# Stage borders of an eight-block network: tile pools placed by lifetime at two ends of SBUF and PSUM, and DRAM sums zeroed in a later stage

## The chip, the cores and the metric

The kernel runs on one core of one Trainium2 chip. The metric is the device time of one execution in microseconds (us). Before the change three executions took 4508.14, 4526.53 and 4512.35 us; the median is 4512.35. One further execution was profiled and took 4548.0 us; all rows of the profile are from that one. TensorE is called PE, VectorE DVE, ScalarE ACT, GpSimd POOL and SyncE SP.

## The reference, cut to what matters

The input is x, 8 sequences of 512 tokens with 128 features, float32. Four layers follow, each an attention block and a feed-forward block, with a norm ahead of each block and its result added to x:

```python
x = x + L0_attn(norm(x))   # delta rule with short convolutions, two FIR filters, a fusing gate
x = x + L0_ffn(norm(x))    # one of 8 experts for each token, weighted by its probability
x = x + L1_attn(norm(x))   # 4 layers: 4 local heads, 4 linear heads, and an MLP each
x = x + L1_ffn(norm(x))    # 8 experts choose their tokens; LayerNorm, MLP, scatter-add
x = x + L2_attn(norm(x))   # gated delta rule, gate, output projection, GELU
x = x + L2_ffn(norm(x))    # 2 layers of windowed attention with rotary positions, and a GLU
x = x + L3_attn(norm(x))   # chunked memory with decay
x = x + L3_ffn(norm(x))    # two of 8 experts for each token
```

What has to start at zero: the expert blocks L1_ffn and L3_ffn add rows into buffers in DRAM (`acc1` and `acc`, two each), which are then added to x.

## The kernel before

**Layout.** x stays in SBUF as 32 tiles of 128 tokens x 128 features (NT = 32), in eight batches of 512 tokens (NB = 8), one for each sequence. `build` (L2035) loads eight constants, calls `load_x` (L74: eight loads of 256 KB on SP's queue) and `row_buffers` (L79), then runs the eight stages as methods one after the other, and stores x.

**DRAM buffers.** `row_buffers` makes `rows_in` (rows that experts gather), `rows_out`, `acc` and `acc1`. It clears a 128 x 1024 tile z on POOL and writes it with POOL-issued DMAs into the extra rows of `rows_in` and over all four sum buffers: 1 + 18 DMAs, 8.5 MB for the 18.

**Stages and pools.** Each stage opens its tile pools in SBUF and PSUM at its begin and closes them at its end. Pools lie on a stack from the left end. So the first pool of a stage gets the addresses of the first pool of the stage before, and a new tile has to wait until whatever lay at its address is done, on every engine and DMA queue that used it. The stages are emitted in program order, and a scheduler then fixes the order of each engine's own queue. An engine executes its queue strictly in order.

The pools that the change names: `a0`, `a0g` and `a0l` of L0_attn (weights and whole-stage tiles; fuse weights; work tiles), with the PSUM rings psA, psC, psD and psF; `f0`, `f0w` and `f0h` of L0_ffn; `a1`, `a1w` and `a1l` of L1_attn; `f1`, `f1s`, `f1w` and `f1h` of L1_ffn (`f1s` holds the norms ahead of the routing); `a2` and `a2l` of L2_attn; `rt` of `route_in` (L611, norm and routing scores of L0_ffn and L3_ffn); `f3`, `f3w` and `f3h` of L3_ffn.

**The norm.** `norm` (L61 to L72) takes one batch of four tiles: four bn_stats (L65) and four bn_aggr (L67) on DVE, `r = var + eps` (L69) on DVE, `r ** -0.5` (L70) on POOL, and four scalings (L72) on DVE.

**Start, L0_attn (L207).** The q, k, v and o projections, the convolution weights and two masks are loaded into `a0`, the fuse weights into `a0g` with their cleared tiles, and softplus of `logit_temp` (L196 to L198, three ACT steps) is worked out for the gate's `tm`. `L0_values` then does, for each batch: norm (xn), transposes, v projection (L276), a causal convolution of four taps on DVE (L187, L189), silu on ACT (L190), and a FIR filter of five taps on DVE (L282, L284).

**L0_ffn (L640) to L1_attn (L694).** The last step of L0_ffn gathers 32 tiles `yg` by indirect DMAs issued on POOL (L609) and adds each, times its probability, to x on DVE (L692). L1_attn opens with three casts of constants, 18 memsets on POOL (L727 to L729: vl, vg, mt, cn, three sets), a norm of each batch into y, and then runs 32 items (4 layers x 8 sequences). `together` (L1535) interleaves four parts of different items by their due times: projection, maxima, values and MLP. Weights of the next layer are loaded through the SP queue one layer ahead (pool `a1w`, two buffers). `L1_maxima` reduces the scores ps_s in PSUM (L845, L847 on PE) into mt by three DVE reduces for an item (L851, L852, L854). With the last layer's MLP, y is finished (L978) and POOL adds it to x (L982).

**L1_attn to L1_ffn (L983).** For each of the eight batches L1_ffn norms x to xn, transposes it and multiplies by the gate, adds xn to x on POOL (L1016), norms xn to yn, and stores yn to `rows_in` (L1019). The norms' tiles are in `f1s`, two buffers each. Then come the choice of tokens, the experts with their scatter-adds into `acc1`, and `add_sums` (L1163): 16 loads `sum` on SP, added to x alternately by DVE and POOL (L1170).

**L1_ffn to L2_attn (L1320).** L2_attn loads some twenty weights and constants, clears the buffers of its triangular inverse (L204, invH), makes two casts (L1346) and `na` (L1348, with an ACT table), and `L2_proj` does for each batch: norm of x to xi, norm of xi to hn, two row operations (L1369, L1370), an RMS norm, transposes, and four projections with convolutions (L1384).

**L3.** L3_attn runs the eight sequences one after the other; L3_ffn loads Wgate, bgate and b3, routes by `route_in`, runs the experts with scatter-adds into `acc`, and ends with `add_sums`.

Of the kernel before, what the change touches and what calls it, by code (L numbers as in the profile page):

```python
# [9 lines left out]
F32 = mybir.dt.float32  # L10
# [5 lines left out]
P = 128  # L16
D = 128
L = 512
TPB = L // P
# [9 lines left out]
class Net:  # L29
# [49 lines left out]
    def row_buffers(self, ctx):  # L79


        tc, nc = self.tc, self.nc
        NR = self.NT * P
        N = ((NR - 8) // 256 + 8) * 256
        dram = ctx.enter_context(tc.tile_pool(name="dram", bufs=1, space=bass.MemoryType.DRAM))
        self.rows_in = dram.tile([NR + P, D], F32, name="rows_in")
        self.rows_out = dram.tile([N, D], F32, name="rows_out")
        self.acc = [dram.tile([NR + P, D], F32, name=f"acc{i}") for i in range(2)]
        self.acc1 = [dram.tile([NR, D], F32, name=f"acc1{i}") for i in range(2)]
        with tc.tile_pool(name="zero", bufs=1) as zp:  # L90
            z = zp.tile([P, 8, D], F32, name="z")
            nc.gpsimd.memset(z, 0.0)
            nc.gpsimd.dma_start(self.rows_in[NR:, :], z[:, 0, :])
            for a in self.acc1 + self.acc:
                N = a.shape[0]
                for n in range(0, N, 8 * P):
                    m = min(8, (N - n) // P)
                    nc.gpsimd.dma_start(a[n : n + m * P, :].rearrange("(t p) d -> p t d", p=P), z[:, :m, :])

# [106 lines left out]
    def L0_attn(self):  # L206
# [4 lines left out]
        H, E, NL = 4, 32, 2  # L211
        with ExitStack() as es:
            cp = es.enter_context(tc.tile_pool(name="a0", bufs=1))
            w = {k: self.load(cp, f"L0_attn_{k}_proj_w", [D, D]) for k in ("q", "k", "v", "o")}
# [10 lines left out]
            ll = cp.tile([P, NT, D], F32, name="ll")  # L225
            gc = es.enter_context(tc.tile_pool(name="a0g", bufs=1))
            lp = es.enter_context(tc.tile_pool(name="a0l", bufs=1))
# [23 lines left out]
            self.ps = es.enter_context(tc.tile_pool(name="ps", bufs=1, space=bass.MemoryType.PSUM))  # L251
            self.rings = {"psA": 1, "psC": 1, "psD": 2, "psF": 2}
            for b in range(NB):
# [356 lines left out]

    def route_in(self, wg, E):  # L611

        nc, NB = self.nc, self.NB
        ps = self.psum("ps_sp")
        with self.tc.tile_pool(name="rt", bufs=3) as rp:
            for b in range(NB):
                xn = rp.tile([P, TPB, D], F32, name="xn")
                self.norm(rp, xn, self.x[:, b * TPB : (b + 1) * TPB, :])
                nc.sync.dma_start(self.seq_rows(self.rows_in, b), xn)
                hT = rp.tile([D, L], F32, name="hT")  # L620
                self.transpose4(hT, xn)
                for t in range(TPB):
                    n = b * TPB + t
                    nc.tensor.matmul(ps[:, n * E : (n + 1) * E], self.cols(hT, t), wg, start=True, stop=True)
        return ps[:, : self.NT * E].rearrange("p (n e) -> p n e", e=E)
# [13 lines left out]
    def L0_ffn(self):  # L639
# [4 lines left out]
        with ExitStack() as es:  # L644
            cp = es.enter_context(tc.tile_pool(name="f0", bufs=1))
            wp = es.enter_context(tc.tile_pool(name="f0w", bufs=5))
            hp = es.enter_context(tc.tile_pool(name="f0h", bufs=2))
            es.enter_context(self.banks(4))
            wr = self.load(cp, "L0_ffn_Wr", [D, E])
            br = self.load_row(cp, "L0_ffn_br", E)  # L650
            lg = self.route_in(wr, E)
            rt = cp.tile([P, NT, E], F32, name="rt")
            nc.vector.tensor_tensor(rt, lg, bc(br, 1, NT), ALU.add)
            nc.scalar.activation(rt, rt, AF.Sigmoid)
            mx = cp.tile([P, NT], F32, name="mx")
            nc.vector.tensor_reduce(mx, rt, AX.X, ALU.max)
# [3 lines left out]
            TB = BS // P  # L660
            idx = self.token_lists(pos, NBLK * TB, cp)
            places = cp.tile([P, NT], mybir.dt.int32, name="places")
            nc.vector.tensor_copy(places, pos)

            st = [{} for _ in range(NBLK)]
            for i in range(NBLK + 2):
# [11 lines left out]
                if 0 <= i - 2 < NBLK:  # L678
                    j = i - 2
                    w, hid = st[j]["w"], st[j]["hid"]  # L680
                    po = self.psum("po")
                    for t in range(TB):
                        for f in range(FC):
                            nc.tensor.matmul(self.cols(po, t), self.cols(hid[:, f, :], t), self.cols(w, FC + f), start=(f == 0), stop=(f == FC - 1))
                    y = hp.tile([P, TB, D], F32, name="y", bufs=3)
                    nc.vector.tensor_copy(y.rearrange("p t d -> p (t d)"), po[:, :BS])
                    nc.sync.dma_start(self.rows_out[j * BS : (j + 1) * BS, :].rearrange("(t p) d -> p t d", p=P), y)
            for n in range(NT):
                yg = hp.tile([P, D], F32, name="yg", bufs=8)
                self.gather(yg, self.rows_out[:, :], places[:, n : n + 1])  # L690
# [3 lines left out]
    def L1_attn(self):  # L694
# [6 lines left out]
        with ExitStack() as es:  # L701
# [36 lines left out]
            for n in range(-2, N + 1):  # L738
                m = n + 2
                if m < N:  # L740
                    i = order[m][0]
# [22 lines left out]
    def single(self, tag, name):  # L764
        return self.ps.tile([P, 512], F32, tag=tag, name=name, bufs=self.rings.get(tag, 2))

# [217 lines left out]
    def L1_ffn(self):  # L984
# [8 lines left out]
        with ExitStack() as es:  # L993
            cp = es.enter_context(tc.tile_pool(name="f1", bufs=1))
            sp = es.enter_context(tc.tile_pool(name="f1s", bufs=2))
            wp = es.enter_context(tc.tile_pool(name="f1w", bufs=3))
# [323 lines left out]
    def L2_attn(self):  # L1320
# [5 lines left out]
        with ExitStack() as es:  # L1326
            cp = es.enter_context(tc.tile_pool(name="a2", bufs=1))
            lp = es.enter_context(tc.tile_pool(name="a2l", bufs=1))
# [32 lines left out]
    def L2_proj(self, s, w, cw, row, col, c, lp):  # L1361
        nc = self.nc
        H = 4
        xb = self.x[:, s["b"] * TPB : (s["b"] + 1) * TPB, :]
        s["xi"] = xi = lp.tile([P, TPB, D], F32, name="xi", bufs=4)
        self.norm(lp, xi, xb)
        hn = lp.tile([P, TPB, D], F32, name="hn")
        self.norm(lp, hn, xi)
        nc.vector.tensor_tensor(hn, hn, bc(row["ln1_g"], 1, TPB), ALU.mult)  # L1369
# [109 lines left out]
    def L2_out(self, s, w, row, col, c, lp):  # L1479
# [40 lines left out]
        hn = lp.tile([P, TPB, D], F32, name="hm")  # L1520
        self.norm(lp, hn, xi)
        yield
# [331 lines left out]
    def L3_ffn(self):  # L1854
# [5 lines left out]
        with ExitStack() as es:  # L1860
            cp = es.enter_context(tc.tile_pool(name="f3", bufs=1))
            wp = es.enter_context(tc.tile_pool(name="f3w", bufs=5))
            hp = es.enter_context(tc.tile_pool(name="f3h", bufs=2))
            es.enter_context(self.banks(8))
            wg = self.load(cp, "L3_ffn_Wgate", [D, E])
            bg = self.load_row(cp, "L3_ffn_bgate", E)
            b3 = self.load(cp, "L3_ffn_b3", [E, D])
            lg = self.route_in(wg, E)
            g = cp.tile([P, NT, E], F32, name="g")
# [168 lines left out]
def build(nc, T, stages, NB, src, dst):  # L2038
    with tile.TileContext(nc) as tc:
        with ExitStack() as ctx:  # L2040
# [11 lines left out]
            net.load_x(src)  # L2052
            net.row_buffers(ctx)
            for s in stages:
                with ExitStack() as es:
# [22 lines left out]
```

## Time and profile before

| What | Value |
|---|---|
| Executions | 4508.14, 4526.53, 4512.35 us; median 4512.35 |
| Profiled execution | 4548.0 us, of which the span of instructions is 4546.2 |
| Mean granted clock of PE | 0.813 |
| Start: window 10 to 40 us | DMA engines 0.94 to 1.03 busy, PE without work until 49.91 |
| L0_ffn to L1_attn | last gathered add 1039.72, PE's next transposes 1068.38 (idle 72.92) |
| L1_attn, window 1840 to 2050 | PE busy 197.32, DVE 102.19, clock 0.98 |
| L1_attn to L1_ffn | last y 2135.95, last of eight norm chains and its row store about 2191 |
| L1_ffn to L2_attn | first sum load 2419.83, PE's first transposes 2457.77 (idle 18.19) |
| L2_attn to L2_ffn | loads 3158.69 to 3174.9, PE on again at 3177.15 (idle 22.63) |
| End | last sums and stores 4511.44 to 4546 |

How to read it: a timeline row gives start, duration, engine, line, operation, output<-inputs with shapes, and in brackets the idle time of that engine just before and what ended it; several like instructions are drawn into one row with their number behind an x. "PEld" is PE's weight load, "SPq" an issue of a DMA on SP. A window row gives each engine's busy time (with the number of its instructions), then the clock granted to PE, the busy share of the 16 DMA engines and GB/s. Line numbers are those of the kernel before; the changed kernel's are 5 higher from L107 on, 6 to 12 higher further down.

### The profile page before, as it was taken

How to read it: one execution, taken by the hardware profiler on the slowest of the kernel's cores; microseconds unless marked ns; L12 is line 12 of the kernel's file. 1: busy time of each engine (PE TensorE's matmuls, PEld its weight loads, DVE VectorE, ACT ScalarE, POOL GpSimd, SP SyncE). 2: the span in 40 equal slices, each digit the busy share in tenths (PEclk: the TensorE clock that was granted, in tenths of full speed). 3: DMA queues.
4: the chain of work that ended last, by engine and by line, in shares of the span. 5: the costliest groups of instructions: out<-in, count | busy, mean ns of one | idle time of the engine just before them, and what ended most of it. 6: DMA issues, size and time to landing. Idle time of an engine off the chain costs nothing.

```text
span 4546.2 us, 104956 instructions
## 1 busy us (share of the span) xinstructions
PE 3767.2 (83%) x45952; PEld 2718.9 (60%) x45952; DVE 2392.7 (53%) x5895; ACT 1687.4 (37%) x2541; POOL 1589.5 (35%) x1575
## 2 busy tenths in 40 slices
PE   3899998575999999997466899995899899986998
PEld 1687776463656565654343677774466566665665
DVE  5445555416454545443615566643766777655333
ACT  2233443112444444442012444532466555631221
POOL 2122221353121112122255334331554554523774
PEclk7565566587999999996576787865899999997998
DMA  3300000150000000000022000001000000001554
GB/s 108 87 3 3 2 3 2 57 151 11 2 5 6 4 7 1 1 1 22 13 50 59 3 3 2 3 3 40 1 1 1 1 1 1 1 13 60 147 147 122
DMA packets 111227, 130.78 MB, mean 29 GB/s; under 512 B 18352, under 2 KB 90497, under 8 KB 110769
## 3 DMA queue, kind: packets, MB, share of 16 engines
q0 software_dynamic: 33184, 76.14, 6.5%
q1 hardware_dynamic: 77584, 47.93, 3.8%
q8 instruction: 361, 5.91, 0.5%
q14 instruction: 98, 0.80, 0.1%
HBM read 96.83 MB, written 27.20 MB: 27 GB/s over the span
## 4 chain that ended last, share of the span: by engine, by line
PE 59%; DVE 18%; ACT 7%; POOL 6%; issue 5%; DMA 2%; another core or an unknown queue 2%; POOLq 0%; SPq 0%; DVEq 0%; ACTq 0%
PE ps_h L971 3%; PE po L977 3%; PE ps_a L1315 2%; POOL nm_r L70 2%; PE ps_qk L1648 2%; PE pd L1279 2%; PE ps_tr L773 2%; PE px L1203 2%; PE pg L1911 2%; PE pz L1210 2%; DVE nm_st L65 2%; PE ps_s L845 2%; DVE mt L854 2%; PE po L1298 1%
## 5 line engine op out<-in xcount | busy, mean ns | idle before, releaser
L70 POOL TENSOR_TENSOR nm_r<-nm_r,mhalf 128x4 f32<-128x4 f32 x168 | 173.0, 1030 | 403.7 <-DVE nm_r L69 399.6
L1660 POOL TENSOR_TENSOR r<-r,rot 128x512 f32<-128x512 f32 x128 | 162.6, 1271 | 303.8 <-DVE rot L1659 248.1
L978 DVE TENSOR_TENSOR y<-y,po 128x512 f32<-128x512 f32 x32 | 22.0, 687 | 313.1 <-PE po L977 313.1
L876 POOL TENSOR_TENSOR cn<-cx,rc 64x448 f32<-64x448 f32 x32 | 37.6, 1174 | 412.9 <-DVE rc L874 412.9
L971 PE MATMUL ps_h<-hTm,w 128*128 128x512 f32 x256 | 163.5, 724 | 11.4 <-ACT hid L972 4.7
L927 ACT ACTIVATE pT<-ps_s 128x2048 f32<-128x2048 f32 x64 | 106.5, 1664 | 169.9 <-PE ps_s L925 169.9
L1648 PE MATMUL ps_qk<-wqkv,hTq 128*128 128x512 f32 x256 | 147.7, 672 | 18.2 <-DVE hTq L1640 7.7
L1199 POOL TENSOR_TENSOR iM<-iN,c_lvl 128x512 f32<-128x512 f32 x64 | 87.1, 1370 | 198.5 <-PE px L1203 185.8
L923 PE MATMUL ps_s<-qa,kT 32*128 32x256 f32 (+1 forms) x1024 | 149.8, 409 | 0.6 <-DVE mt L854 0.3
L609 POOL DMA_INDIRECT xr<-rows_in,tl_idx x124 | 118.7, 957 | 75.7 <-PE pt L634 20.9
L606 POOL DMA_INDIRECT acc<-y,tl_idx x78 | 124.8, 1601 | 45.1 <-DVE y L1921 21.4
L972 ACT ACTIVATE hid<-ps_h,b 128x512 f32<-128x512 f32 x128 | 88.0, 687 | 129.2 <-PE ps_h L971 128.0
L977 PEld LDWEIGHTS po<-w,hid 128*128 128x128 f32 x1024 | 122.2, 199 | 20.9 <-ACT hid L972 20.9
L977 PE MATMUL po<-w,hid 128*128 128x128 f32 x1024 | 128.3, 286 | 5.8 <-ACT hid L972 1.6
L773 PE MATMUL ps_tr<-ident,xn 128*128 128x128 f32 x160 | 29.8, 315 | 124.5 <-DVE xn L72 124.5
L1678 POOL TENSOR_TENSOR r<-r,rn 128x512 f32<-128x512 f32 x128 | 129.1, 1042 | 1.9
L1210 PE MATMUL pz<-iTT,iX 32*32 32x32 f32 x8192 | 103.8, 209 | 25.8 <-issue 19.3
L1210 PEld LDWEIGHTS pz<-iTT,iX 32*32 32x32 f32 x8192 | 92.6, 121 | 54.0 <-issue 36.7
L1650 ACT ACTIVATE sq<-ps_qk 128x512 f32<-128x512 f32 x128 | 75.8, 592 | 121.2 <-PE ps_qk L1648 121.2
L854 DVE TENSOR_REDUCE mt<-ps_s 128x8 f32<-128x2048 f32 x32 | 73.4, 2293 | 88.4 <-PE ps_s L847 88.4
L1203 PEld LDWEIGHTS px<-iT,iM 32*32 32x32 f32 x8192 | 96.2, 126 | 36.6 <-issue 23.1
L1203 PE MATMUL px<-iT,iM 32*32 32x32 f32 x8192 | 106.2, 214 | 5.6 <-issue 3.4
(672 smaller groups left out, 10765.3 us busy)
## 6 DMA issues: line engine op xcount, KB each, us to landing
acc<-z POOLq DMA_DIRECT2D x16, 512.0 KB
fcur<-in_L_attn_fir_cur SPq DMA_DIRECT2D x32, 256.0 KB
sum<-acc SPq DMA_DIRECT2D x32, 256.0 KB
rows_in<-xn SPq DMA_DIRECT2D x16, 256.0 KB
rows_out<-y SPq DMA_DIRECT2D x23, 128.0 KB
x<-in_L_attn_hidden_states SPq DMA_DIRECT2D x8, 256.0 KB
fprev<-in_L_attn_fir_prev SPq DMA_DIRECT2D x8, 256.0 KB
w<-in_L_attn_W SPq DMA_DIRECT2D x8, 256.0 KB
```

What stands on the lines that cost most here:

```text
L70: nc.gpsimd.tensor_tensor(r, r, self.mhalf[:, :G], ALU.pow)
L606: self.nc.gpsimd.indirect_dma_start(out=dst, out_offset=bass.IndirectOffsetOnAxis(ap=idx, axis=0), in_=src, in_offset=None, compute_op=ALU ...
L773: nc.tensor.transpose(self.cols(ps, g), src[:, g, :], self.ident)
L854: nc.vector.tensor_reduce(m4, s4, AX.X, ALU.max, negate=True)
L923: nc.tensor.matmul(ss[:, h, n * 256 : n * 256 + W], kT[R[h], k * P : (k + 1) * P], qa[R[h], k * P : k * P + W], start=True, stop=False)
L971: nc.tensor.matmul(ps, self.cols(w["w1"], f), hT, start=True, stop=True)
L977: nc.tensor.matmul(self.cols(po, t), self.cols(hid[:, f, :], t), w["w2"][:, f, :], start=(f == 0), stop=(f == FC - 1))
L1203: nc.tensor.matmul(px[p, g * B : (g + 1) * B], nm[p, g, :], Ti[p, g, :], start=True, stop=True)
L1210: nc.tensor.matmul(pz[p, g * B : (g + 1) * B], X[p, g, :], TT[p, g, :], start=True, stop=True)
L1648: nc.tensor.matmul(ps, self.cols(hT, t), w["qkv"][:, j, :], start=True, stop=True)
L1660: nc.gpsimd.tensor_tensor(r3, r3, m, ALU.add)
L1678: nc.gpsimd.tensor_tensor(r3, r3, bc(rn[:, j, t, :], 2, E), ALU.mult)
```

## The change

It edits where pools are opened and which pool a tile comes from, and moves the zeroing of the sums; no arithmetic is changed.

- `row_buffers` clears only a 128 x 128 tile and the extra rows of `rows_in`. The new `zero_sums` clears a 128 x 8 x 128 tile z on POOL and writes it over `acc1` and `acc` by 18 DMAs on SP's queue; L1_attn calls it with its pool `a1` when its loop comes to n = 1.
- These pools open at the right end: `a0`, `a0g`; a PSUM pool "psl" of its own for L0_attn's ring psF; `f0y`, new, for L0_ffn's y, yg, mx and places; `f1s`; `a2` and a new `a2x` with the norms' tiles and xi of L2_attn; `rt` (for L3_ffn), `f3`, `f3w`, `f3h`.
- L0_ffn's Wr and br come from the pool of constants.
- `single` takes a ring given as (buffers, pool).

```diff
         with tc.tile_pool(name="zero", bufs=1) as zp:
-            z = zp.tile([P, 8, D], F32, name="z")
+            z = zp.tile([P, D], F32, name="z")
             nc.gpsimd.memset(z, 0.0)
-            nc.gpsimd.dma_start(self.rows_in[NR:, :], z[:, 0, :])
-            for a in self.acc1 + self.acc:
-                N = a.shape[0]
-                for n in range(0, N, 8 * P):
-                    m = min(8, (N - n) // P)
-                    nc.gpsimd.dma_start(a[n : n + m * P, :].rearrange("(t p) d -> p t d", p=P), z[:, :m, :])
+            nc.gpsimd.dma_start(self.rows_in[NR:, :], z)
+
+    def zero_sums(self, pool):
+        nc = self.nc
+        z = pool.tile([P, 8, D], F32, name="z")
+        nc.gpsimd.memset(z, 0.0)
+        for a in self.acc1 + self.acc:
+            N = a.shape[0]
+            for n in range(0, N, 8 * P):
+                m = min(8, (N - n) // P)
+                nc.sync.dma_start(a[n : n + m * P, :].rearrange("(t p) d -> p t d", p=P), z[:, :m, :])
...
-            cp = es.enter_context(tc.tile_pool(name="a0", bufs=1))
+            cp = es.enter_context(tc.tile_pool(name="a0", side="right", bufs=1))
...
-            gc = es.enter_context(tc.tile_pool(name="a0g", bufs=1))
+            gc = es.enter_context(tc.tile_pool(name="a0g", side="right", bufs=1))
...
-            self.rings = {"psA": 1, "psC": 1, "psD": 2, "psF": 2}
+            last = es.enter_context(tc.tile_pool(name="psl", side="right", bufs=1, space=bass.MemoryType.PSUM))
+            self.rings = {"psA": 1, "psC": 1, "psD": 2, "psF": (2, last)}
...
+            yp = es.enter_context(tc.tile_pool(name="f0y", side="right", bufs=3))
             es.enter_context(self.banks(4))
-            wr = self.load(cp, "L0_ffn_Wr", [D, E])
-            br = self.load_row(cp, "L0_ffn_br", E)
+            wr = self.load(self.const, "L0_ffn_Wr", [D, E])
+            br = self.load_row(self.const, "L0_ffn_br", E)
...
-                yg = hp.tile([P, D], F32, name="yg", bufs=8)
+                yg = yp.tile([P, D], F32, name="yg", bufs=8)
...
             for n in range(-2, N + 1):
                 m = n + 2
+                if n == 1:
+                    self.zero_sums(cp)
...
-            sp = es.enter_context(tc.tile_pool(name="f1s", bufs=2))
+            sp = es.enter_context(tc.tile_pool(name="f1s", side="right", bufs=2))
...
-            cp = es.enter_context(tc.tile_pool(name="a2", bufs=1))
+            cp = es.enter_context(tc.tile_pool(name="a2", side="right", bufs=1))
+            self.late = es.enter_context(tc.tile_pool(name="a2x", side="right", bufs=1))
...
-        s["xi"] = xi = lp.tile([P, TPB, D], F32, name="xi", bufs=4)
-        self.norm(lp, xi, xb)
+        s["xi"] = xi = self.late.tile([P, TPB, D], F32, name="xi", bufs=4)
+        self.norm(self.late, xi, xb)
...
-            cp = es.enter_context(tc.tile_pool(name="f3", bufs=1))
-            wp = es.enter_context(tc.tile_pool(name="f3w", bufs=5))
-            hp = es.enter_context(tc.tile_pool(name="f3h", bufs=2))
+            cp = es.enter_context(tc.tile_pool(name="f3", side="right", bufs=1))
+            wp = es.enter_context(tc.tile_pool(name="f3w", side="right", bufs=5))
+            hp = es.enter_context(tc.tile_pool(name="f3h", side="right", bufs=2))
```

## Prediction, made blind

> **What bounds the kernel now.** I read the page's busy shares and its chain first, then windows over each stage border, then the timelines at those borders, and last how the two programs order each engine's instructions.
>
> ```profile
> span 4546.2 us, 104956 instructions
> PE 3767.2 (83%) x45952; PEld 2718.9 (60%) x45952; DVE 2392.7 (53%) x5895; ACT 1687.4 (37%) x2541; POOL 1589.5 (35%) x1575
> PE 59%; DVE 18%; ACT 7%; POOL 6%; issue 5%; DMA 2%; another core or an unknown queue 2%; POOLq 0%; SPq 0%; DVEq 0%; ACTq 0%
> ```
>
> TensorE carries the chain inside the stages; DVE, ACT and POOL carry most of the rest, and the borders are where TensorE stands. The change adds no arithmetic: TensorE's and DVE's instructions stay the same in number, ACT gets three table loads, SP 18 DMAs that POOL loses. TensorE's order is nearly untouched; the other engines' moves lie almost all at borders, so the working goes border by border. The profiled run took 4548.0 us (span 4546.2), 35.7 above the median 4512.35 of the three runs shown; I sum differences from the profiled execution and take them off that median.
>
> **A. The start.** Windows (busy PE, PEld, DVE, ACT, POOL, then clock, DMA share, GB/s) and timeline rows:
>
> ```profile
> 10.00:20.00 10.00, 0.00 (x0) 0.00 (x0) 1.32 (x9) 0.00 (x0) 5.00 (x7) 1.00 1.03 310
> 20.00:30.00 10.00, 0.00 (x0) 0.00 (x0) 0.87 (x4) 0.00 (x0) 5.40 (x8) 1.00 1.03 301
> 2.91 8.86 POOL L98 DMA_DIRECT2D acc<-z  x10
> 4.51 32.69 SPq L77 DMA_DIRECT2D x<-in_L_attn_hidden_states  x8
> 46.66 0.43 SPq L150 DMA_DIRECT2D L_attn_v_proj_w<-in_L_attn_v_proj_w  x1
> 59.28 0.49 DVE L187 TENSOR_SCALAR cv_acc<-cv_pre,L_attn_v_conv_w 128x512 f32<-128x512 f32 x1
> ```
>
> The DMA engines are full with 8.5 MB of zeros (L98); each of the 8 loads of x takes 4.09 us (32.69 / 8), and all compute engines stand. The weights of L0_attn follow on SP, so the first convolution starts at 59.28; from there DVE is busy for 58.33 of 65 us (60 to 125).
> Afterwards only 64 KB of zeros precede x, and the projection weights come directly after x, ahead of the fuse weights. Alone, loads of x's shape go at 1.07 us each (sum<-acc, 8 in 8.56) to 1.35 (out_x<-x, 5 in 6.74): x is issued by 4.51 + 8.6 to 10.8 = 13.1 to 15.3. v_proj is third after it (0.47 apart), the v conv weights seventh; a small load lands about 2.0 us after its issue, so they are there at 16.4 to 18.6 and 18.4 to 20.5. The first norms need 7.5 (first x) to 14.5 (second xn, at the 3.1 us a batch of 50.66 to 57.05). v_proj, 2.05 with its copy and wait as before, is hidden in that: first convolution at 19.5, a gain of 39.8 (38.7 to 40.8). Against it: DVE has by then done 2 xn, 4 statistics, 4 aggregates and the three tm steps less than before, 2.5 us that now fall into its full stretch. On ACT the logit_temp chain (47.08 to 49.03 before, in the idle start) now stands between the first and second silu, waits for a load issued 23rd after x (lands about 26) and brings 3 table loads of 1.28; ACT was idle 4.0 and 4.7 us around those silus, so I take 1 of the 3.84. Sum **-36**; bounds -28 (slow loads, all table loads and waits paid) and -41.
>
> **B. L0_attn to L0_ffn (820 to 855).** The order doesn't change; Wr is loaded earlier, but was there in time (issued 820.97, used 826.41). 0.
>
> **C. L0_ffn to L1_attn (995 to 1068).** After the last gathered add (1039.72), 18 memsets hold POOL from 1040.26 to 1045.5, and the first norm's power waits for them (1045.51). Ten move ahead of the 32 gathers, into POOL's idle time before 998.5 (the gathers may start 0.6 later); eight short ones stay, 1.9 us, so the power starts at about 1040.1. The statistics of four batches go between adds that the gathers pace at 1.25 us. -5.4 + 0.6 = **-5** (-3 to -6).
> The zeroing comes back here: 18 SP DMAs after the first two layers' weights, 8.5 MB at the start's 300 GB/s = 28 us, about 1045 to 1075. Queued behind them on SP is only the third layer's first load, wanted at 1237 before. No other data moves then; only instruction fetch (queue q8, 5.91 MB in the whole run) shares the engines. No row shows it squeezed: 0 to +5, I take **+1**, since TensorE starts only at 1068.
>
> **D. L1_attn to L1_ffn (1950 to 2190).** The interesting border.
>
> ```profile
> 2135.95 0.69 DVE L978 TENSOR_TENSOR y<-y,po 128x512 f32<-128x512 f32 x1 [19.56 <-PE po L977]
> 2136.55 0.87 DVE L65 BATCH_NORM_STATS2 nm_st<-x 128x6 f32<-128x128 f32 x4
> 2152.81 1.12 DVE L72 TENSOR_SCALAR xn<-x,nm_mv,nm_r 128x128 f32<-128x128 f32 x4 [1.19 <-POOL nm_r L70]
> ```
>
> After the last y, eight batches take 6.67 us each of DVE and POOL norms. With f1s on the far side, both norms of batches 0 and 1 and the statistics of batch 2 move into L1_attn. xn of batch 2 then waits only for the transposes of batch 0 behind the last po, about 2137.3 instead of 2152.81: **-15.5**.
> But they go into DVE's queue just ahead of the maxima mt (L851, L852) of items whose seconds count:
>
> ```profile
> 1957.70 0.68 DVE L851 TENSOR_REDUCE mt<-ps_s 128x4 f32<-128x512 f32 x1
> 1958.30 1.22 DVE L852 TENSOR_REDUCE mt<-ps_s 128x4 f32<-128x1024 f32 x1
> 1960.34 0.71 PE L845 MATMUL ps_s<-kT,qT 32*128 32x256 f32 x8
> 1962.40 2.29 DVE L854 TENSOR_REDUCE mt<-ps_s 128x8 f32<-128x2048 f32 x1 [2.88 <-PE ps_s L847]
> ```
>
> TensorE's third group of scores (1960.34) overwrites the PSUM that the second mt reads, and waits for its end (1959.52): slack 0.8. Inserted ahead: a wait for POOL's x 0.3, statistics 0.95, aggregate and r 0.5, power on POOL 1.2 and 0.6 behind cn, xn 1.05, statistics 0.8, aggregate, r and power 1.75, the first yn 0.25: 7.4. Less 0.8, TensorE stands 6.6 us, at 1960 and again at 1991; the third insertion (statistics only, 1.8) costs 1.0. Everything behind TensorE in this stage waits with it (197.32 of 210 us busy). **+14.2**; at least +4 if the gaps of the rest (6%) take some back, and no less, since DVE cannot pass its own queue.
> Then the clock:
>
> ```profile
> 1084.00:1092.00 8.00, 7.95 (x38) 4.51 (x42) 5.02 (x11) 1.37 (x2) 2.74 (x2) 0.50 0.00 0
> 1100.00:1108.00 8.00, 7.47 (x93) 4.69 (x91) 4.79 (x8) 3.51 (x4) 1.18 (x1) 1.00 0.00 0
> 2060.00:2070.00 10.00, 9.76 (x78) 4.93 (x79) 2.31 (x3) 7.34 (x8) 0.34 (x1) 0.66 0.01 2
> ```
>
> The granted clock stands at 0.50 after idle stretches and takes up to 30 us to come back (1068 to 1100), or dips only briefly (0.66 at 2060, 1.00 by 2070). After a hole of 6.6 us I bound the loss by 0 and 8 us each (16 us at half speed) and take 1.5, nearer to the brief dip: **+3** (0 to +16). D together **+1.5** (-12 to +15).
> The Trainium skill, "TensorE: Matmul & The Clock Gate", section "What's actually happening", says that an idle window of about 3.4 us puts the clock to half and a busy one of that length releases it. By it each hole would cost an estimated 1.7 us, 3.4 in all, and the total would stay within half a us; the slow recovery from 1068 to 1100 is longer than the page has it.
>
> **E. L1_ffn to L2_attn (2440 to 2460).** xi and its statistics now lie where nothing late was: batch 0's statistics and xi go between the sum adds, where DVE idled 1 to 1.6 us each time. L2's weights (SP 2439.65 to 2453.7) are issued in the routing of L1_ffn, ahead of expert weights that wait for TensorE anyway. The casts (1.50 at 2440.53) and invH's memset (0.94 at 2439.78) no longer stand ahead of the last adds. hn, at 2450.08 before, needs the second statistics behind the last sum add (about 2440.9) and a power behind POOL's last add: about 2444. **-6** (-3 to -7).
>
> **F, G, H.** L2_attn to L2_ffn and L2_ffn to L3_attn: the first load still waits for the same last POOL add; 0. L3_attn to L3_ffn: Wgate comes earlier, but the first ps_sp (4113.16) waited only 0.72 for bgate: 0 (-2 to 0).
>
> **Sum:** -36 - 5 + 1 + 1.5 - 6 = -44.5: 4503.5 on the profiled execution, **4468** against the median. All bounds at their ends give about -68 and -14.
>
> **Rivals.**
> 1. *The start keeps its pace*: if SP itself, and not the shared engines, sets 4.09 us a load, only the order of the weights gains. v_proj comes at 38.2 instead of 46.66: -8.5, with DVE's 2.5 and ACT's 1 back -5, total -13.5: 4499. Against it: the 1.07 of the same shape, alone. Chance 0.06.
> 2. *The holes cost more*: 8 us of slow clock each instead of 1.5, and the zeros +5: total -27.5: 4485. The recovery from 1068 speaks for it, the dip at 2060 against. Chance 0.12.
> 3. *The holes cost nothing*: D at -12, total -58: 4454. Chance 0.08.
> 4. *Slower*: in the two holes the clock drops and stays at 0.5 as it does from 2150 to 2230. TensorE's work there would double; each us of low clock loses 0.5. With -47.5 from the rest it turns slower from 95 us of low clock, and all 176 us from 1960 to 2136 would give +40: 4553. Busy as TensorE is there (94%), no row shows this. Chance 0.03.
> That it does not do what it says holds for F and G already.
>
> **How the numbers follow.** Forecast (-30 to -55) 0.71, rivals as given. The range 4444 to 4495 takes in rivals 2 and 3, and the median's own spread; it leaves out rivals 1 and 4 and some tails. This kernel's measurement can tell about 0.5% (22.6 us) from no change: faster 0.87 (forecast, rival 3 and most of 2), same 0.09, slower 0.04.
>
> **What would show it.** A: first cv_acc at 18 to 22, loads of x near 1.1 us each. C: first L1_attn norm power right after the gathers. D: TensorE idle about 6 us ahead of L845 in two items near the end of L1_attn, ended by mt; xn of the third batch within 2 us of the last y. E: first transpose of L2_attn 6 us sooner after the last sum. It would be wrong if the first x loads stay at 4 us, or if the windows of L1_attn show a lower clock throughout.

## The result, and the profile after

Over 14 executions of each kernel on the same chip the changed kernel takes 4472.89 us (4448.58 to 4503.43) and the kernel before 4517.22 (4508.14 to 4534.62): a ratio of 0.9903, 95% interval 0.9885 to 0.9921, which is 44 us less (36 to 52). The forecast was 44.5 less. The profiled execution took 4472.09, right at the median; that of the kernel before (4548.0) is slower than all of its 14. The two profiles therefore differ by 76 us, of which about 32 are more than the executions show for the change. The page of the changed kernel:

```profile
span 4470.3 us, 104902 instructions
PE 3750.4 (84%) x45952; PEld 2708.4 (61%) x45952; DVE 2393.0 (54%) x5895; ACT 1690.7 (38%) x2544; POOL 1575.8 (35%) x1558
PE 61%; DVE 18%; ACT 7%; issue 6%; POOL 5%; DMA 1%; another core or an unknown queue 1%; SPq 0%; POOLq 0%; DVEq 0%; ACTq 0%
```

TensorE's and DVE's counts are the same and the shares nearly so: the gain must lie in waits, not in work, and is looked for stage by stage. Lines of the changed kernel stand 5 to 12 higher than before's.

**The start.** Windows with the columns shown before, then rows of the timeline (the durations on SPq are the time that the issues take on SP's queue):

```profile
10.00:20.00 10.00, 6.86 (x13) 3.30 (x14) 7.16 (x34) 3.04 (x4) 2.27 (x3) 1.00 0.57 135
20.00:30.00 10.00, 3.83 (x16) 2.51 (x15) 9.96 (x32) 6.56 (x9) 1.51 (x4) 0.72 0.17 28
```
```profile
4.54 5.71 SPq L77 DMA_DIRECT2D x<-in_L_attn_hidden_states  x8
11.58 0.43 SPq L155 DMA_DIRECT2D L_attn_v_proj_w<-in_L_attn_v_proj_w  x1
18.39 0.49 DVE L192 TENSOR_SCALAR cv_acc<-cv_pre,L_attn_v_conv_w 128x512 f32<-128x512 f32 x1 [0.88 <-ACT cv_pre L190]
...
983.79 28.32 SPq L103 DMA_DIRECT2D acc<-z  x18
```

The loads of x take 0.71 us each (5.71 / 8) instead of 4.09, v_proj is issued at 11.58 instead of 46.66, and DVE's first convolution starts 40.9 us sooner. The zeroing stands in L1_attn now, on SP from 983.79.

**L1_attn.** TensorE's third group of scores (L856, before L845) now waits for the second mt (L863), with the early norms of L1_ffn (xn, its statistics, yn) ahead of it in DVE's queue:

```profile
1868.01 1.11 DVE L72 TENSOR_SCALAR xn<-x,nm_mv,nm_r 128x128 f32<-128x128 f32 x4 [1.13 <-POOL nm_r L70]
1869.04 0.86 DVE L65 BATCH_NORM_STATS2 nm_st<-xn 128x6 f32<-128x128 f32 x4
...
1871.69 0.34 DVE L72 TENSOR_SCALAR yn<-xn,nm_mv,nm_r 128x128 f32<-128x128 f32 x1 [1.13 <-POOL nm_r L70]
1871.95 0.68 DVE L862 TENSOR_REDUCE mt<-ps_s 128x4 f32<-128x512 f32 x1
1872.55 1.22 DVE L863 TENSOR_REDUCE mt<-ps_s 128x4 f32<-128x1024 f32 x1
1873.91 1.23 PE L856 MATMUL ps_s<-kT,qT 32*128 32x256 f32 x8 [6.37 <-DVE mt L863]
...
1946.96 0.71 PE L856 MATMUL ps_s<-kT,qT 32*128 32x256 f32 x8 [1.21 <-DVE mt L863]
```

A hole is a stretch in which TensorE stands. The first is 6.37 us long, the one behind it 6.44 (in the item that ends at 1939), the third 1.21. The eight matmuls behind the first hole take 1.23 us where the same eight take 0.71 in the third item: half speed. How long half speed lasted, in windows of the same profile (the last three columns are granted clock, DMA share, GB/s):

```profile
1874.00:1878.00 4.00, 4.00 (x29) 2.51 (x30) 1.10 (x4) 0.00 (x0) 0.00 (x0) 0.52 0.21 66
1956.00:1966.00 10.00, 9.63 (x61) 6.07 (x59) 4.69 (x17) 4.70 (x8) 3.27 (x3) 0.52 0.01 2
1966.00:1976.00 10.00, 10.00 (x23) 3.54 (x22) 0.13 (x1) 2.15 (x4) 0.00 (x0) 0.50 0.00 0
```

After the first hole the clock is at half until 1878 (0.52 in the first row). From 1956 it stays at half for over 20 us, with TensorE busy throughout (9.63 and 10.00 of 10) and no wait above 1.21 us in the item. The experiments return to that.

**The borders.** Rows of the timeline at the begin of L1_attn, L1_ffn and L2_attn. Where two fences follow each other, the first is of the kernel before (for L1_ffn its rows stand in the prediction). From the last gathered add to the first psq of L1_attn it takes 25.11 us instead of 30.86:

```profile
1039.72 0.35 DVE L692 SCALAR_TENSOR_TENSOR x<-yg,mx,x 128x128 f32<-128x128 f32 x1 [0.85 <-DMA yg<-rows_out,places]
1070.58 2.07 PE L791 MATMUL psq<-hT,wq 128*128 128x512 f32 x2 [0.99 <-ACT hT L777]
```
```profile
982.16 1.69 DVE L699 SCALAR_TENSOR_TENSOR x<-yg,mx,x 128x128 f32<-128x128 f32 x1
1007.27 2.07 PE L802 MATMUL psq<-hT,wq 128*128 128x512 f32 x2 [0.99 <-ACT hT L788]
```

The third batch's xn now starts 2.1 us after the last y (16.9 before), and TensorE's first transposes of L2_attn follow the end of POOL's last add (2388.15 + 1.26) by 8.81 us instead of 13.80 (2457.77 behind 2442.71 + 1.26):

```profile
2442.71 1.26 POOL L1170 TENSOR_TENSOR x<-x,sum 128x512 f32<-128x512 f32 x1 [0.77 <-DVE x L1170]
2457.77 1.08 PE L773 MATMUL ps_tr<-ident,hn 128*128 128x128 f32 x4 [18.19 <-DVE hn L1377]
```
```profile
2097.36 0.69 DVE L989 TENSOR_TENSOR y<-y,po 128x512 f32<-128x512 f32 x1 [19.40 <-PE po L988]
2099.43 0.41 DVE L72 TENSOR_SCALAR xn<-x,nm_mv,nm_r 128x128 f32<-128x128 f32 x1 [1.39 <-PE ps_tr L134]
...
2388.15 1.26 POOL L1181 TENSOR_TENSOR x<-x,sum 128x512 f32<-128x512 f32 x1 [1.23 <-DVE x L1181]
2398.22 1.08 PE L784 MATMUL ps_tr<-ident,hn 128*128 128x128 f32 x4 [11.67 <-DVE hn L1389]
```

### The profile page after: what moved, and what is told of

Same layout as the page of the kernel before. It is cut to its first block, busy times and chain, and to the rows that moved or that the text cites. A ratio compares the mean times of both kernels' runs of the same rounds, so it can differ in the third digit from the quotient of the medians.

```text
span 4470.3 us, 104902 instructions
## 1 busy us (share of the span) xinstructions
PE 3750.4 (84%) x45952; PEld 2708.4 (61%) x45952; DVE 2393.0 (54%) x5895; ACT 1690.7 (38%) x2544; POOL 1575.8 (35%) x1558
## 4 chain that ended last, share of the span: by engine, by line
PE 61%; DVE 18%; ACT 7%; issue 6%; POOL 5%; DMA 1%; another core or an unknown queue 1%; SPq 0%; POOLq 0%; DVEq 0%; ACTq 0%
PE ps_h L982 4%; PE po L988 3%; PE ps_a L1326 2%; POOL nm_r L70 2%; PE pd L1290 2%; PE pg L1923 2%; PE px L1214 2%; PE pz L1221 2%; PE ps_qk L1660 2%; DVE nm_st L65 2%; PE ps_s L856 2%; PE ps_tr L784 2%; DVE mt L865 2%; PE ps_s L934 2%; PE po L1309 1%
## 5 line engine op out<-in xcount | busy, mean ns | idle before, releaser
L1728 DVE TENSOR_REDUCE mx<-ps_s 128x8 f32<-128x1024 f32 x64 | 77.8, 1215 | 62.1 <-PE ps_s L1725 62.1
```

## The experiments

All are measured against runs of the kernel before on the same chip, with a ratio to it and its 95% interval. before_again, gate_b2, gate_b12 and zeros_behind have one execution each, so only their traces are used and no time is read from them. In the table each distance comes from the timeline of one profile: from the first cv_acc to the first ps_f of L0_attn; from there to the first ps_sp of L0_ffn; from the last gathered add to the first psq of L1_attn; the nine distances between the last ten y of L1_attn's items, and their sum; from the last y to the first ps_cnt of L1_ffn; from the end of POOL's last sum add to the first ps_tr of L2_attn.

| kernel | cv_acc | to ps_f | to L0_ffn | C | items near the end of L1_attn | sum | D | E |
|---|---|---|---|---|---|---|---|---|
| before | 59.28 | 63.5 | 703.6 | 30.86 | 32.8 31.2 31.2 31.2 32.8 31.0 28.3 31.6 27.3 | 277.5 | 57.12 | 13.80 |
| before_again | 59.23 | 62.6 | 688.8 | 30.86 | 31.2 31.2 32.8 31.2 31.2 31.0 26.2 29.8 27.1 | 271.9 | 57.10 | 13.81 |
| changed | 18.39 | 61.9 | 686.8 | 25.11 | 31.2 34.4 39.1 39.1 43.0 31.0 27.4 29.8 27.1 | 302.1 | 42.17 | 8.81 |
| zero_late | 19.12 | 64.7 | 692.6 | 31.98 | 31.2 32.8 31.2 31.2 34.4 34.2 26.2 29.7 27.1 | 278.0 | 58.13 | 13.80 |
| pools_only | 64.03 | 64.7 | 690.4 | 23.97 | 31.2 34.4 39.1 39.1 43.0 31.0 27.4 29.8 27.1 | 302.2 | 42.43 | 8.81 |
| f1s_left | 17.48 | 63.0 | 692.6 | 25.70 | 31.2 31.2 32.8 31.2 31.2 31.0 26.2 29.7 27.0 | 271.7 | 58.13 | 8.80 |
| gate5 | 17.89 | 63.5 | 692.4 | 25.10 | 32.8 31.2 31.2 31.2 32.8 31.0 28.3 36.4 26.5 | 281.6 | 42.16 | 8.80 |
| mark3 | 18.45 | 62.4 | 699.1 | 25.12 | 31.2 31.2 34.4 32.8 31.2 31.0 26.2 29.9 27.1 | 275.1 | 35.39 | 8.81 |
| a2_left | 18.04 | 61.7 | 698.0 | 25.12 | 31.2 34.4 39.1 39.1 43.0 31.0 27.4 29.8 27.1 | 302.2 | 42.16 | 13.81 |
| f0_left | 18.20 | 63.1 | 693.1 | 31.99 | 31.2 31.2 39.1 39.1 34.0 31.0 26.2 29.9 27.2 | 289.0 | 42.17 | 8.81 |
| gate_b2 | 18.06 | 63.2 | 694.7 | 25.10 | 31.2 31.2 39.1 39.1 34.4 34.2 26.2 29.6 27.0 | 292.1 | 42.15 | 8.81 |
| gate_b12 | 17.88 | 62.4 | 689.1 | 25.11 | 31.2 31.2 39.1 35.4 31.2 34.2 26.2 33.3 26.9 | 288.8 | 42.15 | 8.80 |
| zeros_behind | 18.15 | 63.0 | 692.6 | 23.97 | 34.4 32.8 39.1 39.1 35.6 31.1 26.2 29.6 27.0 | 294.9 | 42.16 | 8.81 |
| mark3zb | 17.71 | 61.7 | 685.4 | 23.99 | 31.2 34.4 32.8 31.2 31.2 31.0 26.2 29.6 27.0 | 274.8 | 35.45 | 8.81 |

The theory going in: the start gives all of its 41 us, C and E are as forecast, and D loses, because its holes cost more (26 us with the slow clock) than the forecast gave them (17). The rival: the pools carry the 35 us by which the two profiles differ behind the start.

**before_again**: the kernel before, unchanged, for a second profile.

> The kernel before, unchanged, to have a profile of it beside the others of this call. Theory (the 18 us that the changed kernel's profile gained inside L0_attn beyond the start, and the 15 to 20 us that four profiles of the last call gained between 826 and 1070, belong to the execution and the chip, not to the change): against the first profile of before this one is 5 to 15 us shorter inside L0_attn and 10 to 18 shorter between 826 and 1070. Rival (they come from the new order of the start and from the pools): within 3 us of the first profile in both stretches.

Its span is 4489.3, 57 us under the first. L0_attn from ps_f on is 14.8 shorter, and from L0_ffn's first ps_sp to L1_attn's first psq it is 15.3 shorter, with the same 30.86 at C; the changed kernel's profile is as long there as the first one (240.1 with a C that is 5.8 shorter, against 225.0 in a2_left and 225.1 in gate5). So the first profile was slow in places that the change doesn't touch, and the rival loses its 35 us. L0_attn scatters between 685 and 699 in all the kernels but the first profile, with nothing in it that follows the change.

**zero_late** and **pools_only** split the change in two: the zeroing moved with all pools as before, and the pools with the zeroing as before.

```diff
-            z = zp.tile([P, 8, D], F32, name="z")     # zero_late, on the kernel before
+            z = zp.tile([P, D], F32, name="z")
...
+                if n == 1:
+                    self.zero_sums(cp)
```

> The kernel before with one edit: the zeroing of the sums moves from POOL's queue at the start to SP's queue in L1_attn, all pools as before. Theory (the start's gain is the zeroing alone, and the extra 18 us that the changed kernel's profile gains inside L0_attn are the clock of that one execution): first cv_acc at 18 to 20 instead of 59.28, about 41 us less than before, 4472 to 4480; L1_attn's items keep their 31.2 us. Rival (the pools on the far side are needed for the start): weights wait for space as before and the first cv_acc comes after 30. Second rival (the 18 us in L0_attn belong to the new order of the start): 55 to 60 us less than before, about 4460.

> The changed kernel with the zeroing put back to the start on POOL's queue, all pools as changed. Theory (the pools' parts nearly cancel: -4 at L0_ffn to L1_attn, +26 in three holes of L1_attn, -17 behind them, -5 at L1_ffn to L2_attn): 0 against before, between -6 and +6; first cv_acc near 59; two items of L1_attn with 39 us instead of 31. Rival (the 35 us that the two profiles differ by behind the start belong to the pools): 30 us or more less than before, about 4485.

zero_late: 0.9915 (0.9893 to 0.9938), 38 us less. First cv_acc at 19.12 with before's pools; the first rival falls, the second too. pools_only: 1.0006 (0.9983 to 1.0029), no difference from before, as its theory had it. Alone the pools gain nothing: 6.9 at C and 5.0 at E go into D, and the start is 4.8 later (64.03 against 59.28): DVE idles 46.50 us to 54.03, until ACT's step of the logit_temp chain, which stands there ahead of its first statistics.

**f1s_left**, **gate5** and **mark3** ask where D's price lies.

```diff
-            sp = es.enter_context(tc.tile_pool(name="f1s", side="right", bufs=2))
+            sp = es.enter_context(tc.tile_pool(name="f1s", bufs=2))            # f1s_left
...
         st = pool.tile([P, G, 6], F32, name="nm_st", tag="nm_st")              # gate5, in norm
+        if after is not None:
+            nc.gpsimd.tensor_copy(st[:, :, 0:1], after)
...
-                self.norm(sp, xn, xb)
+                self.norm(sp, xn, xb, after=self.x[:, 5 * TPB : 6 * TPB, 0:1] if b < 2 else None)
...
+        if s["i"] == 3 and s["b"] >= 6:                                        # mark3, in L1_mlp
+            self.mark[s["b"]] = mk = self.const.tile([P, TPB, 1], F32, name=f"mark{s['b']}")
+            nc.gpsimd.tensor_copy(mk, xn[:, :, 0:1])
...
-            sp = es.enter_context(tc.tile_pool(name="f1s", side="right", bufs=2))
+            sp = es.enter_context(tc.tile_pool(name="f1s", side="right", bufs=3))
+            sq = es.enter_context(tc.tile_pool(name="f1q", bufs=2))            # for xT, m, part, up
...
+                self.norm(sp, xn, xb, after=self.mark[6] if b < 2 else self.mark[7] if b < 3 else None)
```

> The changed kernel with the pool f1s back on the left, so that the norms of L1_ffn stay behind L1_attn. Theory (the two insertions cost 6.4 us of wait and 1.4 us of slow matmuls each, the third 1.2 and a longer stretch of low clock, 26 in all, and gain 17): all items of L1_attn near 31.2 us, the third batch's xn 16 to 17 us later after the last y, 7 to 11 us less than the changed kernel. Rival (the insertions pay for themselves, as the forecast had it): within 2 us of the changed kernel.

> The changed kernel with f1s on the right as changed, but the statistics of L1_ffn's first two batches wait for the x of the sixth batch (a copy of 128x4 on POOL into the tile of statistics, overwritten by them), so that they come behind the last maxima mt. Theory (the holes come from DVE's order alone and not from the early norms): all items near 31.2 us, the early norms in the last two items, where DVE idled 18 us, xn of the third batch still within 3 us of the last y: 20 to 26 us less than the changed kernel, 4447 to 4453, and less than both kernels. Rival (the norms disturb TensorE wherever they stand): the last two items grow by 6 us each, and 12 us or less are won.

> The changed kernel with f1s on the right as changed, three buffers in it (its transposed tile and the tiles of the bisection in a pool on the left), and the statistics of L1_ffn's first two batches made to wait for the xm of item 7, those of the third for the xm of item 8 (copies of 128x4 on POOL), so that the norms fill the 16 us in which DVE idles behind xm in each of the last two items. Theory (only the place in DVE's queue costs): all items near 31 us, no wait of TensorE for xm (7.01 in the run gate5), and one batch of 6.67 more taken from the border: 34 to 38 us less than the changed kernel, 75 to 82 less than before. Rival (POOL's norms and copies, or xm of the last item, hold TensorE again): no more than gate5's 26.

f1s_left: 0.9883 (0.9856 to 0.9910), 53 us less: 9 better than the changed kernel, as its theory had it, though the two intervals overlap; the trace shows even items (271.7) and the old border (58.13). gate5: 0.9844 (0.9818 to 0.9870), 70 less: the holes are gone (281.6) and the border's gain is kept (42.16). But one item has 36.4 instead of about 30, which is the 6 us of its rival, in one item and not in two, since now the norms stand ahead of that item's xm:

```profile
2023.19 1.15 PE L786 MATMUL ps_tr<-ident,xm 128*128 128x128 f32 x4 [7.01 <-DVE xm L74]
```

mark3 puts them behind xm: 0.9832 (0.9807 to 0.9856), 76 less. TensorE's transposes of xm (first fence) wait 0.93, and the first batch's xn (second fence) starts only behind them:

```profile
2030.39 1.01 PE L787 MATMUL ps_tr<-ident,xm 128*128 128x128 f32 x4 [0.93 <-DVE xm L75]
```
```profile
2035.28 1.11 DVE L75 TENSOR_SCALAR xn<-x,nm_mv,nm_r 128x128 f32<-128x128 f32 x4 [1.15 <-POOL nm_r L73]
```

With a third buffer one more batch is out of the way: the border takes 35.39. So the place in DVE's queue decides and not the norms themselves. That much of the theory holds in all three; in size mark3 is 32 better than the changed kernel, just under the 34 to 38 expected.

**a2_left** and **f0_left** undo E and C alone (pools and tiles of the diff put back on the left).

> The changed kernel with the pools of L2_attn (a2 and the norms' tiles) back on the left. Theory (the working of E): the first transposes of L2_attn come 5 to 6 us later against the last sum's add, nothing else moves, 5 us more than the changed kernel. Rival (L2's first norm is hidden behind its weights anyway): within 1 us at that border.

> The changed kernel with L0_ffn's y, yg, mx, places, Wr and br back in its left pools. Theory (the working of C): ten memsets and the first statistics stand again between the last gathered add and the first norm's power: the first psq of L1_attn 4 to 5 us later, 4 to 5 us more than the changed kernel. Rival (the weights of L1_attn, issued behind the last gather again, land late): 8 us or more.

a2_left: E is back at 13.81, 5.0 more than in the changed kernel; its time, 0.9892 (0.9869 to 0.9915), is too close to the changed kernel's to show 5 us. f0_left: C is at 31.99, 6.9 more where 4 to 5 were expected; 0.9930 (0.9906 to 0.9955), which overlaps the changed kernel's interval too. Neither rival holds.

**gate_b2** and **gate_b12** let only batches 0 and 1, or only batch 0, stay early (gate5's copy for `b == 2`, or for `b in (1, 2)`).

> The changed kernel with only the third batch's early statistics made to wait for the x of the sixth batch, so that the first two insertions stay and the third goes. It asks where the 9 us of slow matmuls in the item behind the third insertion come from (43.0 us in the changed kernel, of which the wait for mt is 1.21). Theory (they belong to the clock after two holes, not to the third wait): items of 39.1, 39.1 and then 40 to 42 us. Rival (the short third wait calls the long stretch): 39.1, 39.1 and then 31 to 33.

> The changed kernel with the second and third batch's early statistics made to wait for the x of the sixth batch: one insertion is left. Theory (a hole costs its wait of 6.4 us and one stretch of 3.4 us of matmuls at half speed): one item of 39.1, all others near 31.2 but for the dips that the kernel before has too. Rival (a hole is followed by a long stretch of half clock): the next item or the one behind it takes 40 us or more.

gate_b2: 39.1, 39.1, then 34.4 and 34.2. The theory's 40 to 42 is wrong, and the rival's 31 to 33 is not met either. gate_b12: one item of 39.1, which is 6.36 of wait and 1.5 more; but the next has 35.4, and another 34.2. The first half of the theory holds, and the rival's 40 doesn't come. Whether the second half holds is open: zero_late, which has no insertion, shows items of 34.4 and 34.2 too. In the windows of gate_b2 in which the changed kernel ran at 0.52 and 0.50:

```profile
1956.00:1966.00 10.00, 9.85 (x38) 5.19 (x37) 3.33 (x11) 3.85 (x6) 1.27 (x2) 0.72 0.01 2
1966.00:1976.00 10.00, 9.81 (x95) 7.35 (x92) 3.27 (x6) 5.19 (x6) 1.27 (x1) 1.00 0.00 0
```

All five kernels with three insertions have the same waits to 0.02 us, and their third item has 43.0 in three of them, 34.0 in f0_left and 35.6 in zeros_behind. So the three waits alone don't call the long stretch at half clock. In all five and in gate_b2 half clock begins at nearly the same place of that item, 43 to 45 us behind the second hole; it lasts 23.9 us in the three kernels with 43.0, 3.4 in f0_left, 6.8 in zeros_behind and gate_b2. One thing goes with the length. In each of the fourteen traces the granted clock changes only on a grid of 3.41 us. In the three kernels with 43.0 the first hole begins 0.04 to 0.08 us ahead of a point of this grid, in f0_left 0.32 and in zeros_behind 1.32 ahead. That fits three kernels which reach the stretch at different times and repeat it item for item. But no run shifts this place alone, and gate_b2, without the third wait, begins 0.07 behind a point. So what sets the length stays open.

**zeros_behind** and **mark3zb** issue the zeroing right behind L0_attn's weights (on the changed kernel and on mark3).

```diff
-                if n == 1:
-                    self.zero_sums(cp)
...
+            self.zero_sums(lp)
             for b in range(NB):
                 self.L0_values(hT[:, b, :], vt[:, 1:, b, :], ls[:, b], w["v"], cw["v"], fs, lp, b)
```

> The changed kernel with the 18 zeroing DMAs issued on SP right behind the weights of L0_attn instead of in L1_attn (from a 128x128 tile of zeros that each DMA reads several times). Theory (at the start the zeros only have to be behind x and the weights; in L1_attn they cost 1 to 2 us): first cv_acc at 18 to 19 as in the changed kernel, L0_attn within its spread of 6 us, the stretch from the first ps_sp of L0_ffn to the first psq of L1_attn 1 to 2 us shorter. Rival (8.5 MB beside the first convolutions hold the loads of fprev and fcur, or the DMA engines): L0_attn 10 us longer or more.

> The kernel mark3 with the zeroing behind the first weights as in zeros_behind: the fastest that these experiments point to. Theory: mark3 less 1 to 2 us, a ratio of 0.980 to 0.986 to before. Rival (the zeros at the start take back the gain there): 0.988 or more.

zeros_behind: first cv_acc at 18.15 and L0_attn as in the others, though its zeros take the DMA engines from 22 to 51; C is 23.97, 1.14 less than in the changed kernel. mark3zb: 0.9812 (0.9778 to 0.9845), 85 us less, the lowest ratio of all; its interval overlaps those of mark3 and gate5, and all three lie clear of the changed kernel's.

The 1.1 at C is not the zeros' traffic but the clearing of their tile on POOL. In the changed kernel (first fence) an add of 0.35 and a norm step of 0.35 take 1.69 and 1.95 while POOL clears z; in zeros_behind (second fence), where z was cleared long before, the same two take 0.34 and 0.35. The delay is complete at 983.85, when the first of the zeros' DMAs (983.79) has only been issued:

```profile
981.90 1.95 DVE L72 TENSOR_SCALAR y<-x,nm_mv,nm_r 128x128 f32<-128x128 f32 x1 [2.25 <-POOL nm_r L70]
982.16 1.69 DVE L699 SCALAR_TENSOR_TENSOR x<-yg,mx,x 128x128 f32<-128x128 f32 x1
...
982.82 0.94 POOL L98 MEMSET z<- 128x1024 f32 x1
```
```profile
973.90 0.35 DVE L72 TENSOR_SCALAR y<-x,nm_mv,nm_r 128x128 f32<-128x128 f32 x1 [2.17 <-POOL nm_r L70]
974.16 0.34 DVE L700 SCALAR_TENSOR_TENSOR x<-yg,mx,x 128x128 f32<-128x128 f32 x1
```

## Why the prediction was right, and where only its sum was

- **A** (-36): the mechanism and the place were right, 18.39 for a forecast 19.5. The measured gain is 41, for the 3.5 us that DVE and ACT were to take back don't show: from cv_acc to ps_f it takes 61.7 to 64.7 in kernels with the early start and 62.6 to 64.7 in those without. DVE's room there (before: 58.33 of 65 us busy) may have taken them up; no run tells. Rival 1 falls with the 0.71 us per load. zero_late shows that the zeroing alone does it.
- **C and the zeros** (-5 and +1): -6.9 and +1.1 at the distance measured. The zeros' price had the right size for the wrong reason: a memset that holds DVE, not DMAs that hold the fetch of instructions.
- **D** (+1.5; its terms add up to 1.7) is the step that was mis-sized, in its clock term. Its three waits were forecast at 6.6, 6.6 and 1.0 and are 6.37, 6.44 and 1.21, one item sooner than forecast (behind the first batch's y, not the second's). The border's gain was forecast at 15.5 and is 15 to 16 (57.1 to 58.1 without the early norms, 42.2 with them). The clock was given 1.5 for each of two holes, 3 together, and nothing behind the third wait. Against 31.2 for an item, the first two of the three items in question lose 1.5 each besides their waits, as forecast; the third loses 10.6, in the 23.9 us at half clock from 1956 on. That is 13.6 for the clock instead of 3. Over all nine items the changed kernel takes 24 to 30 us more than kernels without insertions (302.1 against 271.7 to 278.0), so D is +8 to +15. The 1.5 taken from the dip at 2060 was right for the holes. For a half clock that lasts under a busy TensorE the window from 1084 to 1092 was the row to see (7.95 of 8 us busy, at 0.50). But 1068 to 1100 isn't one slow recovery: the window from 1076 to 1084 has 0.71.
- **E** (-6): -5.0.
- **F, G, H** (0): from L3_attn's first scores (pss) to the end the profiles differ by up to 9.9 us: 491.2 and 487.3 in the two of the kernel before, 485.3 in the changed kernel, 481.3 to 485.2 in the others, with zero_late, which has before's pools, at 484.9. A few us there may be the change's; no run tells.

With the measured sizes the sum is -41 - 5.8 - 5.0 and +8 to +15: 37 to 44 us less, inside the 36 to 52 that the executions show. The total of 44.5 was met because A gave 5 more than forecast and C 2 more, while E gave 1 and D 7 to 14 less: the right side and, in part, luck in the size. Rival 2 had nearly the right total for the clock (16), but in the wrong place: it gave 8 us to each of two holes, which lost 1.5 each.

The Trainium skill, "TensorE: Matmul & The Clock Gate", section "What's actually happening", has half clock after an idle window of about 3.4 us. The first hole agrees: half clock from 1871.0, 3.5 us into the wait of 6.37, until 1877.8, 3.9 us into the matmuls behind it, with 1.5 us lost. At the second hole half clock begins only 1.9 us into the wait (1908.5). The stretch from 1956 on doesn't agree: no idle window of that length is ahead of it (TensorE is busy for 2.21 of the 3.41 us before), and it lasts while TensorE is busy for 23.59 of 23.90 us. By the page the insertions would have cost an estimated 3.4; the profile shows 13.6, and the measurement decides.

## What to carry to other kernels

A pool laid where the last stage is still running lets the next stage start early, and an in-order engine then does that early work wherever the scheduler sees it idle, also a moment before the instruction that TensorE needs. Count what an insertion stands ahead of, and give the early work a dependency on something late enough: here two 128x4 copies (gate5) took both the holes and their slow clock away and kept the border's 15 us, and a later dependency (mark3) also spared the item in which they still stood in the way. Bulk writes with no early reader belong behind the loads that everyone waits for, on whatever queue: before, zeros issued by POOL held the loads on SP (4.09 us each), with the DMA engines at 1.03.

## What the runs showed of the hardware

- Half clock lasted 23.9 us with TensorE busy for 23.59 of them and no idle window of 3.4 us ahead: 1956 to 1980 in the changed kernel, and the same stretch, item for item, in pools_only and a2_left, which reach that point at other times. It is 3.4 and 6.8 us in f0_left and zeros_behind, which have the same waits.
- In all fourteen traces the granted clock changes only on a grid of 3.41 us. L1_attn shows single items of 32.8 to 34.4 instead of 31.2 in kernels without insertions too (32.8 in the kernel before, 34.4 in zero_late), with no new wait of TensorE.
- A memset of 128x1024 on POOL (0.94 us) stretched two operations of DVE from 0.35 to 1.69 and 1.95. The Trainium skill, "SBUF — State Buffer", section "Who interferes with whom", says that certain operations of DVE, tensor_scalar among them, can contend with GpSimd for a shared pair of ports, and that whoever issues first holds the pair for the whole instruction while the other is fully blocked. Both rows end at 983.85, just behind the memset's 983.76, which would agree with L72, a tensor_scalar, being blocked. But L72 starts 0.92 us ahead of the memset's row and usually takes 0.35, so the order of the starts doesn't fit the rule as the rows have it. Whether L699 is blocked itself or only queued behind L72 the rows don't tell.
- Eight loads of x took 0.71 us each on SP's queue with no zeros beside them and 4.09 with 8.5 MB of zeros beside them, which came from POOL's queue.
- Two profiles of one kernel can differ by 57 us of 4500: 15 in L0_attn alone. A difference of stages between two single profiles was no evidence here until a second profile of the kernel before stood beside it.
